# Who empties the bank of the deformable products: VectorE while it combines, or ScalarE behind the products

## The chip, the cores and the metric

The kernel runs on one core of one Trainium2 chip. The metric is the device time of one execution in microseconds (us); the kernel before took 9049.27 us in the median of three runs (9045.97 to 9068.44). Engines are named as the profile names them: PE is TensorE's matmul and PEld its weight load, DVE is VectorE, ACT is ScalarE, POOL is GpSimd, SP is SyncE, which only issues transfers. A `q` behind a name is the engine's sequencer.

## The reference, cut to what matters

Thirty-two images of 96 channels and 56 x 56 points go through two layers. The first is a hidden layer of 576 channels (1x1 convolution, 3x3 depthwise convolution, squeeze and excitation, 1x1 projection, residual). The second weights the image by a channel and a spatial attention, both drawn from its spectrum, and gives `y`. From `y` it computes offsets, a gate, an ordinary 3x3 convolution `y_base` and a deformable one, `y_def`. The part that the change touches is:

```python
sampled = _grid_sample_taps(y, px, py)
y_def = jnp.einsum('bcthw,oct->bohw', sampled, def_w.reshape(c, c, 9))
y_def = y_def + def_b[None, :, None, None]
z = (1 - gate) * y_base + gate * y_def
mu = z.mean((0, 2, 3), keepdims=True)
```

`z` is then normalised over all images, added to the layer's input and cut at zero. Everything is float32.

## The kernel before, in words

**Bands.** An image is cut into 7 bands of 8 rows, 448 points each, so that there are 224 bands. A band is worked in two halves of 7 tiles of 4 x 4 points, two tiles high (`h` = 0 and 1). For each half, sampling is done by products on TensorE (L739) of a transposed block of the image (`yt`, L721 to L727: copied by POOL, transposed by PE, emptied by ACT) with interpolation weights (`wc`, multiplied by DVE at L710 after two loads); ACT copies the results to `v` (L743) and packs two of the nine taps into the idle partitions (L750). Then `deform` (L758) multiplies `v` by the weights of the deformable convolution and adds up seven products in a bank of PSUM.

**The bank.** This bank is a pool of its own, `pd`, with one buffer. The first half of a band opens it, the second half adds its own columns, and then it holds all of the band's `y_def` without its bias. The other users of PSUM share six banks, `mm`, and one, `acc`. So the first products of the next band can't begin before `pd` has been read.

**The combining.** `combine` (L794 to L801) runs on DVE: L797 reads the bank, adds the bias `def_b` and subtracts `yb` (that is, `y_base`) in one instruction that writes `z`; L798 multiplies by the gate plus one; L799 halves and adds `yb`; L800 takes the statistics. `z` comes from a pool of two buffers. POOL stores it (L1061) later, and after the seventh band of an image DVE joins the statistics (L1068).

**The order of the work.** Beside the bands run two other streams: the hidden layer of the image after next (L169 to L262: expansions by PE emptied by ACT at L173, and depthwise taps, mostly on DVE at L262 and L260, closed by ACT at L222) and the attention of the next image (L285 to L587, with reductions on DVE at L379 and L437 that PE waits for at L440). `pump` advances both by a count of slots, 17 to a band, as their steps come due, and also runs what stands in the list `later` with a slot number. The offsets of the band after next (`find`: L615, L635, L637, L644, L649, L664 to L691) go along with them.

The end of a half isn't emitted where the half ends but in the next half, behind the first group of its sampling products: `ends` holds it. `end_half` emits `deform`, and after the second half it puts `join` into `later`, due two slots on. `join` calls `combine` and puts the store off by another seven slots.

What is emitted is not yet the order in which an engine works. When the kernel is built, the framework orders the instructions of each engine by an estimate of when each is ready, with earlier emission as the preference; SP's queue alone is kept as written. After that each engine works through its list strictly in order, and waits at an instruction whose operands or buffer are not there, whatever stands behind it.

Of the kernel before, what the change touches and what calls it, by code (L numbers as in the profile page):

```python
# [9 lines left out]
AF = mybir.ActivationFunctionType  # L10
ALU = mybir.AluOpType
# [5 lines left out]
C, H, W = 96, 56, 56  # L17
# [18 lines left out]
BW = NBW  # L36
# [81 lines left out]
def bank(p):  # L118
    return p["mm"].tile([128, 512], FP, name="mm")
# [485 lines left out]
def load_freq(nc, p, yp, b, r0, r1):  # L605
    nc.sync.dma_start(yp[CA - 1 : CA, PD + r0 : PD + r1, PD : PD + W], p["fq", b][:, r0:r1])


def conv3(nc, out, weights, yp, channels, j):

    view = out.rearrange("p (h w) -> p h w", h=RB)
    for k in range(NTAP):
        dy, dx = divmod(k, 3)
        r0 = j * RB + dy + PD - 1
        nc.tensor.matmul(view, weights[:, k], yp[:channels, r0 : r0 + RB, dx + PD - 1 : dx + PD - 1 + W],  # L615
                         start=(k == 0), stop=(k == NTAP - 1))
# [136 lines left out]
def deform(nc, p, pd, v, h):  # L753

    out = pd[:C, :BW].rearrange("c (q w) -> c q w", q=RB)[:, :, h * W // 2 : (h + 1) * W // 2]
    for k in range(KA):
        ks = slice(0, 128 if k else C)
        nc.tensor.matmul(out.rearrange("c q (t x) -> c t q x", x=TS), p["w"]["def"][ks, k],  # L758
                         v[ks, k].rearrange("c t s (r x) -> c t (s r) x", r=TS),
                         start=(k == 0), stop=(k == KA - 1))  # L760


def gate_of(nc, p, hid):

    pg = bank(p)
    nc.tensor.matmul(pg[:C, :BW], p["w"]["dg2"], hid, start=True, stop=True)
    return gate_from(nc, p, pg)


def gate_from(nc, p, pg):  # L770
    gate = p["q1"].tile([C, BW], FP, name="gate")
    nc.scalar.activation(gate, pg[:C, :BW], AF.Tanh, bias=p["w"]["half"]("dg2_b", C), scale=0.5)
    return gate
# [11 lines left out]
def base_conv(nc, p, j, yp):  # L785

    pb = bank(p)
    conv3(nc, pb[:C, :BW], p["w"]["base"], yp, C, j)
    yb = p["q1"].tile([C, BW], FP, name="yb")
    nc.scalar.activation(yb, pb[:C, :BW], AF.Identity, bias=p["w"]["cv"]("base_b"))  # L790
    return yb


def combine(nc, p, j, pd, yb, gate, st):  # L794

    z = p["q2"].tile([C, BW], FP, name="z")
    nc.vector.scalar_tensor_tensor(z, pd[:C, :BW], p["w"]["cv"]("def_b"), yb, ALU.add, ALU.subtract)  # L797
    nc.vector.scalar_tensor_tensor(z, gate, 1.0, z, ALU.add, ALU.mult)  # L798
    nc.vector.scalar_tensor_tensor(z, z, 0.5, yb, ALU.mult, ALU.add)  # L799
    nc.vector.bn_stats(st[:, j], z)  # L800
    return z  # L801
# [132 lines left out]
def padded(nc, p, a, images):  # L934

    cp = p["cp"]
    yps = [cp.tile([CJ, HY, WY], FP, name=f"yp{i}") for i in range(images)]
    for t in yps:
        nc.gpsimd.memset(t, 0.0)
        nc.sync.dma_start(t[C : C + 4, PD : PD + H, PD : PD + W], a["coord"])  # L940
        nc.sync.dma_start(t[CA:, PD : PD + H, PD : PD + W], a["place"])
    p["s4"] = [cp.tile([H, 3, WP], FP, name=f"s4_{i}") for i in range(2)]
    for t in p["s4"]:
        nc.gpsimd.memset(t, 0.0)
    return yps


def pools(tc, ctx, p, space, sizes):
    for name, bufs in sizes:
        kw = {"space": space} if space else {}  # L950
        p[name] = ctx.enter_context(tc.tile_pool(name=f"l1{name}", bufs=bufs, **kw))


def layers(tc, a, dp, x1d, zd, stats, far):
# [6 lines left out]
    nc = tc.nc  # L961
    B = x1d.shape[0]
    with ExitStack() as ctx:
        p = {"tc": tc, "dp": ctx.enter_context(tc.tile_pool(name="l1d", bufs=3, space=DRAM))}
# [3 lines left out]
        yp, = padded(nc, p, a, 1)  # L968
# [21 lines left out]
        streams, later = [], []  # L990
        slot = 0
# [68 lines left out]
        def store(b, j, z):  # L1060
            nc.gpsimd.dma_start(zd[b][:, j * BW : (j + 1) * BW], z)  # L1061

        def join(n, pd, gate, st):
            b, j = bands[n]
            z = combine(nc, p, j, pd, ybs[n], gate, st)
            later.append((slot + 7, lambda: store(b, j, z)))
            if j == NBD - 1:
                nc.vector.bn_aggr(stats[:, b], st)  # L1068

        def end_half(n, h, v, gate, st):  # L1070
            if h == 0:
                pds[n] = p["pd"].tile([128, 512], FP, name="pd")
            deform(nc, p, pds[n], v, h)
            if h:
                pd = pds.pop(n)
                later.append((slot + 2, lambda: join(n, pd, gate, st)))

        ends, pds = [], {}

# [9 lines left out]
        hids, gates, ybs, hds, ready = [], [], [], [], []  # L1089
# [31 lines left out]
        for n, (b, j) in enumerate(bands):  # L1121
            if j == 0:
                st = p["st"].tile([C, NBD, 6], FP, name="st")
# [7 lines left out]
            for h in range(2):  # L1131
# [20 lines left out]
                if h == 0:  # L1152
                    if n % 2 == 0:
                        gates.extend(gates_of(nc, p, hids[n // 2]))
                    gate = gates.pop(0)
# [108 lines left out]
def gather_block(tc, a, dp, x1d, zd, stats):  # L1264

    nc = tc.nc
    B = x1d.shape[0]
    sd = dp.tile([B, C, 2], FP, name="sd")
    with ExitStack() as ctx:
        p = {"dp": ctx.enter_context(tc.tile_pool(name="l1d", bufs=1, space=DRAM))}  # L1270
        pools(tc, ctx, p, PSUM, (("mm", 7), ("acc", 1)))
        constants(tc, ctx, a, p, True)
        yp, = padded(nc, p, a, 1)
        table = dp.tile([TAB, 4 * C], FP, name="table")
        with tc.tile_pool(name="l1z", bufs=1) as zp:
            zt = zp.tile([116, TAB * C // 116], FP, name="zt")
            nc.gpsimd.memset(zt, 0.0)
            tz = table.rearrange("(p n) f -> p (n f)", p=116)
            for i in range(4):
                nc.sync.dma_start(tz[:, i * zt.shape[1] : (i + 1) * zt.shape[1]], zt)  # L1280
        pools(tc, ctx, p, None, (("ca", 1), ("s1p", 1), ("xc", 2), ("sp", 1), ("sq", 2), ("hq", 1), ("q1", 2), ("q2", 2),
                                 ("hid", 2), ("off", 1), ("ix", 2), ("vp", 1), ("gp", 4), ("smp", 2)))
        with tc.For_i(0, B, 1) as b:
            st = p["sp"].tile([C, NBD, 6], FP, name="st")
            zo = p["dp"].tile([C, HW], FP, name="zo")
            xi = p["dp"].tile([C, HW], FP, name="xi")
            nc.sync.dma_start(xi.unsqueeze(0), x1d[bass.ds(b, 1)])
            for _ in attend(tc, p, 0, None, None, None, xi, True):
                pass
            for q in range(NB):  # L1290
                attend_table(nc, p, yp, table, xi, q)
            load_freq(nc, p, yp, 0, 0, H)
            for j in range(NBD):
                hid, wq, idx = locate(nc, p, yp, j)
                v = p["vp"].tile([C, NTAP, BW], FP, name="v")
                for t in range(GT):
                    sample_table(nc, p, table, wq, idx, v, t)
                pd = bank(p)
                for k in range(NTAP):
                    nc.tensor.matmul(pd[:C, :BW], p["w"]["def"][:, k], v[:, k], start=(k == 0), stop=(k == NTAP - 1))  # L1300
                z = combine(nc, p, j, pd, base_conv(nc, p, j, yp), gate_of(nc, p, hid), st)
                nc.sync.dma_start(zo[:, j * BW : (j + 1) * BW], z)
            mv = p["sp"].tile([C, 2], FP, name="mv")
            nc.vector.bn_aggr(mv, st)
            nc.sync.dma_start(zd[bass.ds(b, 1)], zo.unsqueeze(0))
            nc.sync.dma_start(sd[bass.ds(b, 1)].rearrange("o c n -> (o c) n"), mv)
    nc.sync.dma_start(stats, sd.rearrange("b c s -> c b s"))
# [50 lines left out]
@with_exitstack  # L1358
def body(ctx, tc, a, out):
    nc = tc.nc  # L1360
    B = a["x"].shape[0]
    dp = ctx.enter_context(tc.tile_pool(name="dram", bufs=1, space=DRAM))
    x1d = dp.tile([B, C, HW], FP, name="x1d")
    zd = dp.tile([B, C, HW], FP, name="zd")
    keep = ctx.enter_context(tc.tile_pool(name="keep", bufs=1))
    stats = keep.tile([C, B, 2], FP, name="stats")
    far = keep.tile([NOFF, 1], I32, name="far")
    with tc.manual_schedule(engines={mybir.EngineType.SP}):
        layers(tc, a, dp, x1d, zd, stats, far)

    reg = nc.values_load(far[0:1, 0:1], min_val=0, max_val=1)
    with tc.If(reg > 0):
        gather_block(tc, a, dp, x1d, zd, stats)
    normalise(tc, a, dp, [x1d[b] for b in range(B)], [zd[b] for b in range(B)], stats, out)
# [142 lines left out]
```

## Time and profile before

| what | value |
|---|---|
| median of three runs | 9049.27 us (9045.97 to 9068.44) |
| the profiled execution | 9059.03 us |
| its span, first to last instruction | 9057.2 us |
| mean granted clock of TensorE | 0.939 |
| L797, bank to `z` on DVE | 224 times, 665 / 680 / 690 ns (least, median, most) |
| L798, L799, L800 on DVE | 224 times each, medians 621, 614, 619 ns |
| L637 and L772 on ACT, bank to SBUF, 448 columns | 224 times each, 627 and 625 ns |
| DVE waiting at L797 for the products (L758) | 166.1 us in 64 waits, 8.1 at most |
| TensorE waiting at L758 for L797 | 115.6 us in 26 waits, 6.1 at most |
| TensorE busy, 1000 to 8000 us | 940 to 949 us of each 1000 |
| last product / end of span | about 8769 us / 9057 us |

How to read it: the span begins with some 500 us of constants and the first image, and ends with 285 us of normalisation, in which TensorE does nothing and transfers bound the time. Between them the same image step of about 264 us repeats, so that a view of one step (the timeline) stands for all, and totals over the span are divided by some 30 images. "Busy" is the time in which an engine had an instruction running; "idle before" is the time it stood still just ahead of a group of instructions, with the instruction that ended the wait. PEclk is the clock that TensorE was granted, 1.00 being the full one. In the page's second part each digit is the busy share of a fortieth of the span in tenths.

### The profile page before, as it was taken

The numbers are of one execution on the slowest core, as the hardware profiler recorded it, in microseconds if no ns is written. First come the engines' busy times: TensorE is split into PE (matmuls) and PEld (weight loads), VectorE is DVE, ScalarE is ACT, GpSimd is POOL, SyncE is SP. The second block draws the span as 40 slices with busy tenths as digits, with TensorE's granted clock in tenths as the row PEclk, the third lists the DMA queues.
The fourth block names the chain that finished last, engine by engine and source line by source line (L and its number), as shares of the span: only waits on it lengthen the run. The fifth ranks groups of instructions, "written<-read, shape, count | busy, mean of one in ns | idle before, by whom it ended". The sixth has DMA issues, their size and how long they took to land. (4 is left out here: it accounts for less than half of the span.)

```text
span 9057.2 us, 137476 instructions
## 1 busy us (share of the span) xinstructions
PE 8175.3 (90%) x52406; PEld 5193.5 (57%) x52406; DVE 7184.4 (79%) x6629; ACT 5393.5 (60%) x10486; POOL 2902.8 (32%) x2800
## 2 busy tenths in 40 slices
PE   5889999999999999999999999999999999999960
PEld 3456565665656566565656656565665655566640
DVE  7688888888888888888888888888888888888333
ACT  2356665666666666666666666666666666666553
POOL 0233333333333333333333333333333333333210
PEclk9889999999999999999999999999999999999985
DMA  2356666666666666666666666666666666666669
GB/s 82 108 142 160 163 169 165 157 154 153 163 166 171 166 157 147 158 165 164 172 161 154 159 157 168 165 174 161 154 154 160 165 166 172 166 156 144 144 188 416
DMA packets 1068758, 1486.48 MB, mean 164 GB/s; under 512 B 590191, under 2 KB 839839, under 8 KB 1055807
## 3 DMA queue, kind: packets, MB, share of 16 engines
q1 hardware_dynamic: 858995, 985.20, 46.4%
q10 hardware_dynamic: 153803, 329.80, 10.2%
q0 software_dynamic: 55296, 162.60, 6.7%
q8 instruction: 420, 6.88, 0.4%
q14 instruction: 244, 1.99, 0.1%
HBM read 1064.29 MB, written 412.65 MB: 163 GB/s over the span
## 5 line engine op out<-in xcount | busy, mean ns | idle before, releaser
L262 DVE SCALAR_TENSOR_TENSOR acch<-hp,w,acch 128x1512 f32<-128x1512 f32 (+1 forms) x2250 | 4456.4, 1981 | 141.4 <-ACT hp L173 103.8
L615 PE MATMUL mm<-yp,c_jointW 104*128 104x448 f32 x4032 | 1679.6, 568 | 10.1 <-DMA yp<-fqd 10.1
L758 PE MATMUL pd<-v,c_def 128*96 128x224 f32 (+1 forms) x6272 | 1468.8, 382 | 142.7 <-DVE z L797 115.6
L721 POOL COPY ybl<-yp 96x448 f32<-96x448 f32 x896 | 1048.3, 1198 | 1204.9 <-PE mm L725 1204.8
L758 PEld LDWEIGHTS pd<-v,c_def 128*96 128x96 f32 (+1 forms) x6272 | 1062.2, 176 | 449.8 <-issue 116.9
L615 PEld LDWEIGHTS mm<-yp,c_jointW 104*128 104x128 f32 x4032 | 776.6, 196 | 784.2 <-issue 747.4
L743 ACT COPY v<-mm 96x288 f32<-96x288 f32 (+1 forms) x2688 | 1004.3, 441 | 156.0 <-PE mm L739 109.3
L169 PE MATMUL mm<-xt,w 96*128 96x392 f32 (+3 forms) x2688 | 1058.5, 527 | 35.3 <-DMA xt<-in_x 33.1
L739 PE MATMUL mm<-wc,yt 64*96 64x144 f32 x12544 | 1056.9, 300 | 20.8 <-DVE sq L379 6.7
L739 PEld LDWEIGHTS mm<-wc,yt 64*96 64x96 f32 x12544 | 834.2, 164 | 317.3 <-issue 199.1
L173 ACT ACTIVATE hp<-mm,sh,inv 128x392 f32<-128x392 f32 (+2 forms) x1216 | 810.7, 673 | 344.8 <-PE mm L169 290.5
L710 DVE TENSOR_TENSOR wc<-wc,wr 128x1008 f32<-128x1008 f32 x448 | 566.6, 1265 | 412.5 <-DMA wr<-hd 385.1
L644 PE MATMUL mm<-yp,c_base0W 96*64 96x224 f32 x8064 | 830.1, 358 | 5.7 <-ACT hp L173 5.7
L329 PE MATMUL mm<-hq,w3s 128*96 128x392 f32 x2048 | 749.7, 510 | 63.6 <-DMA hq<-h2d 62.2
L672 POOL DMA_DIRECT2D od<-at x224 | 186.7, 834 | 1908.3 <-DVE at L664 1292.6
L750 ACT COPY v<-v 32x448 f32<-32x448 f32 x1344 | 755.1, 562 | 29.7
L727 ACT COPY yt<-mm 128x384 f32<-128x384 f32 (+1 forms) x896 | 353.9, 439 | 700.7 <-PE mm L725 699.0
L644 PEld LDWEIGHTS mm<-yp,c_base0W 96*64 96x64 f32 x8064 | 555.2, 135 | 282.7 <-issue 61.0
L635 ACT ACTIVATE hid<-mm,c_dg1b 50x448 f32<-50x448 f32 x224 | 140.8, 628 | 868.4 <-PE mm L615 858.4
L476 POOL TENSOR_TENSOR o<-o,xc 96x392 f32<-96x392 f32 x256 | 376.2, 1470 | 806.2 <-ACT o L339 804.2
L222 ACT ACTIVATE acch<-acch,sh,inv 128x1568 f32<-128x1568 f32 x288 | 488.4, 1696 | 202.8 <-DVE acch L262 176.5
L329 PEld LDWEIGHTS mm<-hq,w3s 128*96 128x96 f32 x2048 | 323.0, 166 | 395.2 <-issue 367.5
(194 smaller groups left out, 9325.3 us busy)
## 6 DMA issues: line engine op xcount, KB each, us to landing
h2d<-acch ACTq DMA_DIRECT2D x288, 784.0 KB
wc<-hd SPq DMA_DIRECT2D x896, 252.0 KB
wr<-hd SPq DMA_DIRECT2D x448, 504.0 KB
hq<-h2d SPq DMA_DIRECT2D x128, 980.0 KB
hq<-h2d SPq DMA_DIRECT2D x128, 784.0 KB
hq<-x1d SPq DMA_DIRECT2D x768, 98.0 KB
ht<-od SPq DMA_DIRECT2D x224, 252.0 KB
hd<-ho ACTq DMA_DIRECT2D x224, 252.0 KB
```

Source lines behind the costliest of these rows:

```text
L169: nc.tensor.matmul(pt[p0 : p0 + w1.shape[1], : rows * W], w1, xts[hf][:, r0 * W : (r0 + rows) * W], start=True, stop=True)
L173: nc.scalar.activation(h1[lo:hi, row0 : row0 + rows, 1 : 1 + W], pt[lo:hi, : rows * W].rearrange("p (h w) -> p h w", h=rows), AF.Silu, bia ...
L262: nc.vector.scalar_tensor_tensor(acc[:, lo:hi], win, wk, acc[:, lo:hi], ALU.mult, ALU.add)
L329: nc.tensor.matmul(pts[half][:C, :EW], w3s[:, ch], hq, start=(i == 0), stop=False)
L615: nc.tensor.matmul(view, weights[:, k], yp[:channels, r0 : r0 + RB, dx + PD - 1 : dx + PD - 1 + W], start=(k == 0), stop=(k == NTAP - 1))
L644: nc.tensor.matmul(pb[i * BC : (i + 1) * BC, : BW // 2].rearrange("p (h w) -> p h w", h=RB // 2), w["base"][:, k], yp[:C, r0 + i * RB // 2 ...
L710: p["tc"].keep_in_program_order(nc.vector.tensor_tensor(wc, wc, wr, ALU.mult))
L721: nc.gpsimd.tensor_copy(yb[:, :, s], blocks)
L739: nc.tensor.matmul(pt[k][:C, (t - lo) * KP : (t - lo + 1) * KP], yt[ps, t], s[ps, t * KP : (t + 1) * KP], start=True, stop=True)
L743: nc.scalar.copy(v[:C, :, lo:hi, k].rearrange("c k t p -> c t k p"), pt[k][:C, : (hi - lo) * KP].rearrange("c (t k p) -> c t k p", t=hi - ...
L750: nc.scalar.copy(v[C:, 1 + 2 * i : 3 + 2 * i], v[i * QC : (i + 1) * QC, KA:])
L758: nc.tensor.matmul(out.rearrange("c q (t x) -> c t q x", x=TS), p["w"]["def"][ks, k], v[ks, k].rearrange("c t s (r x) -> c t (s r) x", r=T ...
```

## The change

The reading of the bank is split off from `combine` and given to ScalarE, which adds the bias on the way and writes `z` in SBUF. It is emitted directly behind the products of the second half, no longer with the combining two slots later. `combine` finds `z` in SBUF and subtracts `yb` there, as a plain subtraction of two tiles in SBUF; its other three instructions stay. The slots of the combining and of the store stay as well. `z`'s buffer is taken two slots earlier than before. The second path, `gather_block`, which runs only when an offset is too large for the tiles (it doesn't with these inputs), gets the same two calls.

```diff
-def combine(nc, p, j, pd, yb, gate, st):
+def take(nc, p, pd):
 
     z = p["q2"].tile([C, BW], FP, name="z")
-    nc.vector.scalar_tensor_tensor(z, pd[:C, :BW], p["w"]["cv"]("def_b"), yb, ALU.add, ALU.subtract)
+    nc.scalar.activation(z, pd[:C, :BW], AF.Identity, bias=p["w"]["cv"]("def_b"))
+    return z
+
+
+def combine(nc, p, j, z, yb, gate, st):
+
+    nc.vector.tensor_tensor(z, z, yb, ALU.subtract)
     nc.vector.scalar_tensor_tensor(z, gate, 1.0, z, ALU.add, ALU.mult)
     nc.vector.scalar_tensor_tensor(z, z, 0.5, yb, ALU.mult, ALU.add)
     nc.vector.bn_stats(st[:, j], z)
...
-        def join(n, pd, gate, st):
+        def join(n, z, gate, st):
             b, j = bands[n]
-            z = combine(nc, p, j, pd, ybs[n], gate, st)
+            combine(nc, p, j, z, ybs[n], gate, st)
             later.append((slot + 7, lambda: store(b, j, z)))
...
             deform(nc, p, pds[n], v, h)
             if h:
-                pd = pds.pop(n)
-                later.append((slot + 2, lambda: join(n, pd, gate, st)))
+                z = take(nc, p, pds.pop(n))
+                later.append((slot + 2, lambda: join(n, z, gate, st)))
```

More of the change, by code (lines that the diff above doesn't have):

```diff
@@ L1300, in gather_block @@
                     nc.tensor.matmul(pd[:C, :BW], p["w"]["def"][:, k], v[:, k], start=(k == 0), stop=(k == NTAP - 1))
-                z = combine(nc, p, j, pd, base_conv(nc, p, j, yp), gate_of(nc, p, hid), st)
+                z = take(nc, p, pd)
+                combine(nc, p, j, z, base_conv(nc, p, j, yp), gate_of(nc, p, hid), st)
                 nc.sync.dma_start(zo[:, j * BW : (j + 1) * BW], z)
```

## The prediction

> **What bounds the kernel now.** I read the page first (busy shares and slices), then the list of waits of TensorE, then the timeline around the longest of them, then short windows with the granted clock.
>
> ```profile
> PE 8175.3 (90%) x52406; PEld 5193.5 (57%) x52406; DVE 7184.4 (79%) x6629; ACT 5393.5 (60%) x10486; POOL 2902.8 (32%) x2800
> ...
> PE   5889999999999999999999999999999999999960
> ...
> DVE  7688888888888888888888888888888888888333
> ```
>
> From the fourth slice to the last but two TensorE is busy nine tenths or more (windows of 1000 us between 1000 and 8000 give 940 to 949), VectorE eight tenths; ScalarE has 616 to 636 of each 1000. TensorE is the bound, and what can be won is its idle time of 50 to 60 us in each 1000, and time in which its clock is low. The waits of TensorE, columns total us, times, longest:
>
> ```profile
> PE pd L758 <- DVE z L797: 115.6, 26, 6.1
> PE acc L440 <- DVE m_fy L437: 72.8, 30, 5.6
> PE acc L440 <- DVE m_fe L437: 71.1, 31, 2.5
> PE mm L329 <- DMA hq<-h2d: 62.2, 31, 4.2
> PE mm L725 <- DVE at L664: 57.2, 28, 5.7
> PE pd L758 <- ACT v L743: 19.3, 36, 2.8
> ```
>
> The largest is the one that the change touches: the first product of a new band waits until VectorE's L797 has read the only bank of `pd`. It strikes 26 times in 224 bands, about once per image. The timeline shows one (start, duration, engine):
>
> ```profile
> 4748.53 2.81 PE L758 MATMUL pd<-v,c_def 96*96 96x224 f32 x14
> ...
> 4751.71 0.78 ACT L727 COPY yt<-mm 128x384 f32<-128x384 f32 x2 [2.25 <-PE mm L725]
> ...
> 4752.44 1.21 DVE L710 TENSOR_TENSOR wc<-wc,wr 128x1008 f32<-128x1008 f32 x1 [4.91 <-DMA wr<-hd]
> ...
> 4753.56 5.92 DVE L262 SCALAR_TENSOR_TENSOR acch<-hp,w,acch 128x1568 f32<-128x1568 f32 x3
> ...
> 4756.18 1.74 ACT L750 COPY v<-v 32x448 f32<-32x448 f32 x3
> ...
> 4759.52 0.68 DVE L797 SCALAR_TENSOR_TENSOR z<-pd,c_cvec,yb 96x448 f32<-96x448 f32 x1
> ...
> 4760.25 1.06 PE L758 MATMUL pd<-v,c_def 96*96 96x224 f32 x2 [3.80 <-DVE z L797]
> ...
> 4761.74 4.42 PE L758 MATMUL pd<-v,c_def 128*96 128x224 f32 x12
> ```
>
> The old band's products end at 4751.34. VectorE first waits 4.91 us for a load, then runs L710 and three taps of 5.92 us, and reads the bank only at 4759.52; TensorE has stood still for 3.80 us. And there is a second price. The 14 products at 4748.53 took 2.81 us, 0.201 each; the 12 behind the stall took 4.42, 0.368 each. The windows tell why (length, then busy time by engine, then PEclk, the granted clock):
>
> ```profile
> 4754.00:4756.45 2.45, 2.45 (x18) 1.23 (x18) 2.42 (x2) 2.42 (x4) 0.07 (x1) 1.00 0.51 103
> 4756.45:4760.25 3.80, 0.00 (x0) 0.00 (x1) 3.68 (x3) 3.73 (x8) 0.00 (x0) 0.83 1.02 318
> 4760.25:4766.00 5.75, 5.75 (x19) 4.52 (x20) 5.63 (x10) 0.72 (x2) 0.52 (x1) 0.52 1.00 211
> ```
>
> Clock 1.00 before, 0.83 over the stall, 0.52 over the next 5.75 us of full work: the stall halves the clock and work behind it pays.
>
> **The change part by part.** *The stall.* The bank is now freed by one ScalarE instruction, emitted directly behind the products and not two slots later. In the example ScalarE had 2.25 us free until 4751.71, and the products end at 4751.34 in that gap: the copy would run from about 4751.4 to 4752.0 and push the row behind it by 0.34. TensorE, idle from 4756.45, needs for the next products only `v`. Its first tap uses rows written by L743 long before; the taps behind it need L750, which ends at 4757.92 for all three packs, 4758.3 with the push, the first pack over a microsecond earlier; four transposes stand in between. I leave 0.5 us of the stall per place. 26 waits give 115.6 - 13 = 103 us.
>
> *The clock behind it.* I laid 27 windows of 14 us at these places, 1305 to 8194. TensorE is idle for 114.9 of their 378 us. Their clocks are 0.76 seventeen times, 0.88 twice, 0.63 to 0.67 eight times, mean 0.733: half clock for (1 - 0.733) x 2 x 378 = 202 us, 7.5 per place. In the example 1.3 of its 6.8 us of half clock lie in the stall and 5.5 in work, which at 0.368 for 0.201 holds 3.0 us of full-clock work: 2.5 us lost. Scaled by 7.5/6.8 to 27 places: some 70 us. It goes if the stall goes, since in the window before it the clock is 1.00. Together 103 + 70 = 173 us, 6.4 per image.
>
> *ScalarE's new work.* 224 instructions from PSUM, 96 x 448 with a bias. Nearest row: L637, the same operation with 32 x 448, 627 ns; L772 with 96 x 448, 625. So 224 x 0.63 = 141 us on an engine that is idle for 37% of the steady part. Identity with a bias is used by L637, L649 and L339 today, and no table load (131 in all, 1283 ns) stands at those lines, so I add none. On the path: the copy is emitted just ahead of the second group of L743, on which L758 waits 36 times already. All waits of TensorE for ScalarE sum to about 75 us in some 70 times. Bounds: nothing, and 141 if each copy delays TensorE in full. I take 20, which lengthens 70 such waits by 0.3 each, since most lines of ScalarE wait for TensorE themselves (L635 858 us, L727 699).
>
> *VectorE.* L797 goes (680 ns in the median), a subtraction with both operands in SBUF comes.
>
> ```profile
> L798 DVE SCALAR_TENSOR_TENSOR z<-gate,z 96x448 f32<-96x448 f32 x224 | 196.1, 876 | 3.7
> L799 DVE SCALAR_TENSOR_TENSOR z<-z,yb 96x448 f32<-96x448 f32 x224 | 152.2, 679 | 2.4
> L797 DVE SCALAR_TENSOR_TENSOR z<-pd,c_cvec,yb 96x448 f32<-96x448 f32 x224 | 152.2, 679 | 170.3 <-PE pd L758 166.1
> ```
>
> L798 and L799 read both operands from SBUF: median 621 and 614, yet up to 1870 and 970; L797 reads one from PSUM and stays within 665 to 690 in all 224. So the subtraction costs VectorE between 224 x (614 - 680) = -15 and 224 x (876 - 679) = +44 us; I take L799's mean, which gives nothing. This row is where a rule speaks against the change: "SBUF — State Buffer" of the Trainium skill, section "Who interferes with whom", says that a VectorE instruction with two SBUF inputs contends with a GpSimd instruction that reads SBUF, one blocking the other, while one with a single SBUF input does not. By the rule the subtraction becomes like L798 and the sum is worse by what part of 44 us reaches TensorE; by L799 it is unchanged. The spreads above agree with the rule.
>
> VectorE also waits differently: 64 times, 166.1 us, it stood at L797 for the products; now it stands some 0.7 us longer, 45 us in all. None of this holds the bank any more, and nothing of VectorE's z chain is read by TensorE; what it delays is what is queued behind it (L262, L437, L664). The store on POOL (L1061) waits for L799 as before and has nothing urgent behind it: z has two buffers and is written some 38 us apart, so taking it two slots earlier costs nothing.
>
> *What is late next.* With 6.4 us gained per image TensorE comes sooner to its other waits for VectorE. Behind the stall VectorE is busy 42.18 of 50 us (4760 to 4810), then 82.01 of 90 (to 4900), then 66.60 of 86. So it has 7.8 + 8.0 us of slack up to the place where L725 waits for L664 and L440 for L437, of which part is waiting for loads, that do not come sooner. There some of the lead is lost. Bounds: nothing given back, and all. VectorE's slack to 4986 is 35 us against 6.4 wanted, nearer to nothing, but the tight stretch (4810 to 4900) comes first: I take 40%, 70 us.
>
> **Sum.** -103 - 70 + 20 + 0 + 70 = -83 us. The profiled execution took 9059.0 (span 9057.2 and 1.8 around it), 9.8 above the median of 9049.3; so 8976 for it and 8966 by the median.
>
> **Rivals.** *(a) All of it arrives.* Nothing is given back and ScalarE's copies are hidden: 9049 - 173 = 8876. For: VectorE's slack over a whole image; against: 91% in the tight stretch. 0.2.
>
> *(b) The bank comes no earlier, or the next wait takes it all.* The order on each engine is fixed when the program is built, by estimates. If the copy is put behind L222, L750 and the gates (until 4759.1 in the example), the bank is free at 4759.8, as late as now; or L437 and L664 hand back everything. Then 9049 - 173 + 173 and 0 to 20 of copies: about 9050 to 9070, say 9055. Against: the copy's emission ahead of those lines. 0.12.
>
> *(c) Slower: ScalarE blocks in front of the products.* ScalarE works in order. If its queue reaches the copy before the products are done, it stands, and behind it stand the emptyings of the six banks of `mm` (L743, L727, L173), for which TensorE waits next. VectorE shows how often the queue is early: 64 times, 166.1/64 = 2.6 us each. The price is 64 x (2.6 + 0.63) = 207 us if nothing hides it, against the 103 won with the rest given back: from half of it reaching TensorE the change loses. In full 9049 - 103 + 207 = 9153; at two thirds, which I take for it, 9049 - 103 + 138 = 9084. For: the products of one half stretch to over 16 us in some bands, interleaved with other work. Against: ScalarE stands 858 us at L635 today and TensorE does not mind. 0.13.
>
> **How the numbers follow.** The forecast, 8966, has a chance of 0.55, (a) 0.2, (b) 0.12, (c) 0.13. Its own range by the unknown costs is 8920 to 9020. The range from 8870 to 9085 takes in (a) and (b) and (c) at two thirds, and leaves out about 0.15: (c) in full, and a new order of all queues, which any edit brings. A measurement here tells apart about 0.3%, 27 us. Faster by more than that: (a), and nearly all of the forecast: 0.74. Within: (b) and the forecast's edge: 0.12. Slower: (c) and a little of (b): 0.14.
>
> **What would show it.** The wait of L758 for z must vanish from TensorE's list, and the one for the new copy be under 20 us; the clock over the steady part rise from 0.96 (0.95 to 0.96 in windows of 1000 us) to 0.97 or more; ScalarE's busy time rise by 141. The give-back shows as larger waits of L440 and L725 for VectorE. A new line of ScalarE waiting for L758 with over 150 us, and L743 among the first that TensorE waits for, is (c). The prediction is wrong if the stalls go and the time stays.

## The result and the profile after

The kernel after takes 8973.95 us in the median of four runs (8964.88 to 8983.66), the kernel before beside it 9051.45 (9045.97 to 9068.44): a ratio of 0.9911, 95% interval 0.9893 to 0.993. That is 78 us less; the forecast was 83 less. The profiled execution took 8980.98 us, against 9059.03 before. Its busy shares, and TensorE's waits (total us, times, longest):

```profile
PE 8127.0 (91%) x52406; PEld 5153.6 (57%) x52406; DVE 7147.7 (80%) x6629; ACT 5486.5 (61%) x10710; POOL 2988.3 (33%) x2800
```

```profile
PE acc L440 <- DVE m_fe L437: 70.6, 31, 2.5
PE acc L440 <- DVE m_fy L437: 70.6, 29, 8.9
PE mm L739 <- DVE sq L379: 59.8, 29, 3.5
PE mm L329 <- DMA hq<-h2d: 57.8, 30, 3.8
...
PE mm L725 <- POOL ybl L721: 39.6, 37, 3.0
...
PE pd L758 <- ACT v L743: 23.9, 34, 1.3
PE mm L396 <- DVE sq L379: 20.6, 17, 2.5
...
PE mm L725 <- DVE at L664: 7.8, 10, 1.4
```

Two things are to be seen. The wait of L758 for the bank, 115.6 us before, is gone without a successor of its own. And three waits have grown most: for L379 (6.7 before, all at L739), for POOL's L721 (1.0 before) and, lower in the list, L615 for a load (30.5, before 10.1). The same work of TensorE, 52406 products, takes 8127.0 us instead of 8175.3; by the clock records of the two traces, 565 us of it ran at half clock, before 702.

The place of the old stall, in the timeline (the combining's lines are now L803 to L806, the copy is L797):

```profile
4698.17 2.81 PE L758 MATMUL pd<-v,c_def 96*96 96x224 f32 x14
...
4701.02 0.63 ACT L797 ACTIVATE z<-pd,c_cvec 96x448 f32<-96x448 f32 x1 [1.92 <-PE pd L758]
...
4702.17 1.90 DVE L710 TENSOR_TENSOR wc<-wc,wr 128x1008 f32<-128x1008 f32 x1 [4.24 <-DMA wr<-hd]
...
4703.99 5.61 DVE L262 SCALAR_TENSOR_TENSOR acch<-hp,w,acch 128x1568 f32<-128x1568 f32 x3
...
4705.93 0.54 PE L758 MATMUL pd<-v,c_def 96*96 96x224 f32 x2
...
4706.64 2.44 PE L758 MATMUL pd<-v,c_def 128*96 128x224 f32 x12
```

VectorE has a like load wait and the same three taps in front of it, but ScalarE has the bank empty at 4701.65, in the gap ahead of L727. The next products start at 4705.93 with no wait, and the twelve take 2.44 us, not 4.42. Some 30 us on, a new one stands (two windows: length, busy times, granted clock):

```profile
4735.62 1.83 DVE L262 SCALAR_TENSOR_TENSOR acch<-hp,w,acch 128x1568 f32<-128x1568 f32 x1
...
4737.48 0.62 DVE L379 TENSOR_REDUCE sq<-mm 112x56 f32<-112x448 f32 x1
...
4738.16 1.14 PE L739 MATMUL mm<-wc,yt 64*96 64x144 f32 x8 [2.27 <-DVE sq L379]
```

```profile
4736.00:4738.16 2.16, 0.00 (x0) 0.00 (x0) 2.13 (x3) 0.62 (x2) 2.16 (x3) 1.00 0.36 85
4738.16:4742.00 3.84, 3.84 (x24) 3.07 (x28) 2.96 (x4) 2.36 (x6) 0.22 (x1) 0.52 0.61 152
```

L379 reduces squares out of a bank of `mm`; it is queued behind a tap, and L739 needs that bank. Here 2.27 us and the clock's halving are paid again. The list above has 29 waits of this kind, about one per image. So the stall was in part exchanged for a shorter one.

### The profile page after: what moved, and what is told of

It is laid out like the page before. It is cut to its first block, busy times and chain, and to the rows that moved or that the text cites. A ratio compares the mean times of both kernels' runs of the same rounds, so it can differ in the third digit from the quotient of the medians.

```text
span 8979.2 us, 137810 instructions
## 1 busy us (share of the span) xinstructions
PE 8127.0 (91%) x52406; PEld 5153.6 (57%) x52406; DVE 7147.7 (80%) x6629; ACT 5486.5 (61%) x10710; POOL 2988.3 (33%) x2800
## 5 line engine op out<-in xcount | busy, mean ns | idle before, releaser
L615 PE MATMUL mm<-yp,c_jointW 104*128 104x448 f32 x4032 | 1669.5, 565 | 31.5 <-DMA yp<-fqd 30.5
L721 POOL COPY ybl<-yp 96x448 f32<-96x448 f32 x896 | 1137.6, 1297 | 1080.7 <-PE mm L725 1080.4
L758 PE MATMUL pd<-v,c_def 128*96 128x224 f32 (+1 forms) x6272 | 1400.0, 369 | 25.6 <-ACT v L743 23.9
L615 PEld LDWEIGHTS mm<-yp,c_jointW 104*128 104x128 f32 x4032 | 772.1, 195 | 802.8 <-issue 764.5
L758 PEld LDWEIGHTS pd<-v,c_def 128*96 128x96 f32 (+1 forms) x6272 | 1024.7, 170 | 304.3 <-issue 82.1
L739 PE MATMUL mm<-wc,yt 64*96 64x144 f32 x12544 | 1053.3, 298 | 73.2 <-DVE sq L379 59.8
L743 ACT COPY v<-mm 96x288 f32<-96x288 f32 (+1 forms) x2688 | 1004.1, 443 | 116.8 <-PE mm L739 91.2
L739 PEld LDWEIGHTS mm<-wc,yt 64*96 64x96 f32 x12544 | 827.3, 162 | 367.4 <-issue 194.3
L710 DVE TENSOR_TENSOR wc<-wc,wr 128x1008 f32<-128x1008 f32 x448 | 586.3, 1309 | 403.9 <-DMA wr<-hd 377.5
L750 ACT COPY v<-v 32x448 f32<-32x448 f32 x1344 | 755.2, 562 | 29.6
L169 PEld LDWEIGHTS mm<-xt,w 96*128 96x128 f32 (+1 forms) x2688 | 363.0, 179 | 327.8 <-issue 222.5
```

The lines of the kernel that those rows point to most:

```text
L169: nc.tensor.matmul(pt[p0 : p0 + w1.shape[1], : rows * W], w1, xts[hf][:, r0 * W : (r0 + rows) * W], start=True, stop=True)
L710: p["tc"].keep_in_program_order(nc.vector.tensor_tensor(wc, wc, wr, ALU.mult))
L721: nc.gpsimd.tensor_copy(yb[:, :, s], blocks)
L739: nc.tensor.matmul(pt[k][:C, (t - lo) * KP : (t - lo + 1) * KP], yt[ps, t], s[ps, t * KP : (t + 1) * KP], start=True, stop=True)
L743: nc.scalar.copy(v[:C, :, lo:hi, k].rearrange("c k t p -> c t k p"), pt[k][:C, : (hi - lo) * KP].rearrange("c (t k p) -> c t k p", t=hi - ...
L750: nc.scalar.copy(v[C:, 1 + 2 * i : 3 + 2 * i], v[i * QC : (i + 1) * QC, KA:])
```

## The experiments

My theory: the change wins because the only bank of `pd` no longer waits for VectorE's late queue, and what is lost again is lost where VectorE is late with another bank. Rivals: the earlier emission does it, whichever engine reads; or it is no more than a new order of the queues, which any edit brings.

### Which engine, or which moment

`dve_behind`, the kernel before with VectorE's reading emitted directly behind the products:

```diff
             if h:
-                pd = pds.pop(n)
-                later.append((slot + 2, lambda: join(n, pd, gate, st)))
+                z = take(nc, p, pds.pop(n), ybs[n])   # L797's instruction, on VectorE
+                later.append((slot + 2, lambda: join(n, z, gate, st)))
```

> The kernel before, with VectorE's reading of the bank (pd plus bias minus yb, one instruction) emitted directly behind the products and the rest of the combining two slots later as before. The engine stays, only the moment moves. Theory 'engine' (the bank came late because VectorE's queue runs late, and ScalarE's doesn't): the wait of L758 for z stays above 60 us, time 9000 to 9060. Rival 'moment' (the earlier emission alone frees the bank): the wait falls under 30 us, time 8990 or less.

Measured: 9196.76 us, ratio 1.0167 (1.0151 to 1.0182). Neither expectation held. The wait of L758 for `z` is gone, as the rival said, and yet the time is 1.7% longer. VectorE now reaches L797 too early and stands there for the products (the first line), and TensorE has a new wait (the second):

```profile
DVE z L797 <- PE pd L758: 351.7, 97, 8.0
...
PE mm L739 <- ACT v L750: 99.9, 51, 4.9
```

Before, these were 166.1 us in 64 waits and 5.9 us in two. What is queued behind L797 comes late, and TensorE pays for it: at the old place L739 starts at 4808.17 after 2.37 us of standing, 0.10 behind the end of L710 (4806.88, 1.19 long), which multiplies its weights and follows L797 on VectorE. (The list puts this wait down to ScalarE's L750.) TensorE's busy time also rose, from 8175.3 to 8263.1 us. This is the mechanism of rival (c) of the prediction, on VectorE.

`act_late`, the kernel after with ScalarE's copy emitted with the combining, two slots later:

```diff
-                z = take(nc, p, pds.pop(n))
-                later.append((slot + 2, lambda: join(n, z, gate, st)))
+                pd = pds.pop(n)
+                later.append((slot + 2, lambda: join(n, pd, gate, st)))   # join calls take
```

> The kernel after, with ScalarE's copy of the bank emitted with the combining, two slots later. The engine is changed, the moment isn't. Theory 'engine': the wait of L758 for the copy stays under 20 us, and the time within 25 us of the kernel after (8950 to 9000). Rival 'moment': the wait comes back with over 60 us, time 9010 to 9060.

Measured: 8976.61 us, ratio 0.9923 (0.991 to 0.9936); no wait of L758 for the copy. These are the numbers of theory 'engine', but the run is no test of the moment, for the planner put the copy back:

```profile
4711.40 0.63 ACT L797 ACTIVATE z<-pd,c_cvec 96x448 f32<-96x448 f32 x1 [1.92 <-PE pd L758]
4711.93 0.76 ACT L727 COPY yt<-mm 128x384 f32<-128x384 f32 x2
```

It stands where it stood in the kernel after, behind the same 1.92 us of waiting for the products and ahead of L727. So it is in nearly every band: ahead of L727 189 times, in the kernel after 191, and in both kernels 0.04 us behind the last product in the median. `act_late` is thus the kernel after once more. What a later copy on ScalarE would cost stays open; that an earlier reading doesn't help on VectorE is what `dve_behind` shows.

### Freeing the bank without ScalarE, and ScalarE without freeing the bank

`two_banks` and its control `five_banks`:

```diff
-        pools(tc, ctx, p, PSUM, (("mm", 6), ("acc", 1), ("pd", 1)))
+        pools(tc, ctx, p, PSUM, (("mm", 5), ("acc", 1), ("pd", 2)))   # control: 5, 1, 1
```

> The kernel before with two banks for the deformable products and five for the rest instead of one and six; VectorE empties them as before. To be read against five_banks. Theory 'the bank' (what the change wins is that the next products need not wait for VectorE): the wait of L758 for z is under 15 us, half clock is less, and the time is 60 to 110 us below five_banks. Rival 'a new order of the queues, or VectorE's shorter work': within 20 us of five_banks.

> Control for two_banks: the kernel before with five banks of mm instead of six, and one for the deformable products; one bank of PSUM lies idle. Both theories: the wait of L758 for z stays at 90 to 140 us; the time is 0 to 80 us above the kernel before (9050 to 9130), by waits for mm banks.

Measured: `five_banks` 9013.84 us, ratio 0.9959 (0.9943 to 0.9975); `two_banks` 8998.44, ratio 0.9954 (0.9939 to 0.9968). Two surprises. With a bank less for everything else the kernel was not slower but 0.4% faster, although its L758 still waits 95.9 us for `z`. And freeing the bank on top won 15 us, nothing that the intervals can tell apart, although that wait is gone; the rival expected this, my theory 60 to 110. Where it went:

```profile
PE mm L739 <- DVE sq L379: 44.2, 19, 5.3
...
PE mm L615 <- DVE sq L379: 34.2, 16, 3.6
```

In `five_banks` these are 10.3 and 0.9. So in the profiled executions (that of `two_banks` is the fastest of its six) 67 of 96 us came back at L379's banks, as in the kernel after.

`both_read`, the kernel before with ScalarE's copy added; VectorE reads the bank as well and overwrites `z`:

```diff
+    nc.scalar.activation(z, pd[:C, :BW], AF.Identity, bias=p["w"]["cv"]("def_b"))   # behind the products
...
     nc.vector.scalar_tensor_tensor(z, pd[:C, :BW], p["w"]["cv"]("def_b"), yb, ALU.add, ALU.subtract)
```

> The kernel before, with ScalarE's copy of the bank into z added behind the products as in the kernel after; VectorE then reads the bank itself as before and writes z anew. ScalarE's work of the change is there, the early release of the bank isn't. Theory 'the bank': the wait of L758 for VectorE's z stays at 80 to 140 us, half clock as before, time 9040 to 9100 (ScalarE's 141 us cost 0 to 50). Rival 'a new order' (the gain comes from how the queues fall out once ScalarE has these rows): 8960 to 9010 although the bank is held.

Measured: 9094.47 us, ratio 1.0055 (1.0042 to 1.0068), with

```profile
PE pd L758 <- DVE z L803: 112.8, 28, 5.9
```

Time and wait lie where my theory put them. ScalarE's new work with the bank still held costs 43 us. The gain is not ScalarE's presence in the order; between this kernel and the one after, 120 us apart, lie the release of the bank and the simpler first instruction of VectorE.

### What order alone can do

`before_slot3` and its pair `after_slot3`, and `after_slot4`: the combining is due three (four) slots behind the products.

```diff
-                later.append((slot + 2, lambda: join(n, pd, gate, st)))
+                later.append((slot + 3, lambda: join(n, pd, gate, st)))
```

> The kernel before with the combining due three slots behind the products and not two: an edit that frees nothing sooner. It samples what a new order alone can do, since five banks in place of six made the kernel faster by 0.4%. Theory 'the bank': the bank is freed later, the wait of L758 grows from 116 to 130 to 250 us, time 9060 to 9150. Rival 'a new order': anything within 60 us of the kernel before on either side, with no relation to that wait.

> The kernel after, with the combining due three slots behind the products and not two; ScalarE's copy stays directly behind the products. The pair to before_slot3 (9004), which won 47 us by order alone with the stall still there at 121 us. Theory 'the bank': the stall's worth comes on top, 50 to 110 us below before_slot3: 8895 to 8955. Rival 'a new order' (the change won its 78 us by an order of the same kind, and both can't be had): within 25 us of the kernel after or slower, 8960 or more.

> The same with four slots. Theory 'the bank': z has nothing waiting for it but the store, so the time stays within 40 us of after_slot3, and the wait of L758 for the bank stays under 20 us. Rival 'a new order': anywhere from 8900 to 9050, with the spread that three slots against two had.

Measured: `before_slot3` 9004.14 us, 0.9951 (0.9938 to 0.9964), against my theory: it wins 47 us while L758 waits 120.7. Its waits of L440 for L437 (m_fy) are 10.7 us, before 72.8, but others grew as much, POOL's L721 from 1.0 to 62.1; the gain is in TensorE's busy time, 8124.6 us against 8175.3. `after_slot3` takes 8968.09, 0.9901 (0.9885 to 0.9918), `after_slot4` 8969.58, 0.9901 (0.9885 to 0.9917). Between the two with three slots the release is worth 36 us by the medians (45 by the ratios), half of the 78 at two slots, and less than the 50 that I asked of the bank: the rival's line, 8960 or more, is the one that held. `after_slot4` stays as near to `after_slot3` as theory 'the bank' said (no wait of L758 for the bank), but it lies in the rival's range too. `after_slot3` is the fastest median of all, but its interval overlaps with that of the kernel after.

### Where the rest went back

`squares`, the kernel after with L377's squares in SBUF, and `before_squares`, the same edit of the kernel before:

```diff
-        sq = bank(p)[: 2 * H, : CG * W].rearrange("h (c w) -> h c w", c=CG)
+        sq = p.get("o", p["xc"]).tile([2 * H, W, CG], FP, name="o").rearrange("h w c -> h c w")
```

> The kernel after, with the squares of L377 written to a tile in SBUF (channels innermost) and not to a bank of mm; VectorE reduces them from there. So no bank of the six waits for VectorE's L379 any more. Theory 'handed back' (what the freed bank won was partly lost where VectorE, running late, holds mm banks at L379): the waits of L739 and L396 for L379, 80 us together, go, and 30 to 80 us are won: 8895 to 8945. Rival 'VectorE itself is late' (another wait for it takes their place, L437, L664 or POOL's L721): within 25 us of the kernel after.

> Control for squares: the kernel before with the same edit. There L379 cost TensorE 7 us. Theory 'handed back': the wait of L758 for z stays over 80 us and the time within 40 us of the kernel before. Rival 'the squares' banks matter by themselves': 40 to 100 us faster than before.

Measured: 9056.32 us, 1.0012 (1.0 to 1.0025), and 9069.48, 1.0028 (1.0017 to 1.004). Neither expectation of `squares` held. The waits for L379 did go, but the edit is no clean test. L377, writing rows with the channels innermost, takes 1030 ns instead of 547, it waits 129.9 us for loads at a worse place of ScalarE's queue (9.9 in the kernel after), and stalls of mostly 3 to 5 us stand near the old place again, now put down to ScalarE:

```profile
PE pd L758 <- ACT v L743: 80.4, 51, 5.0
...
PE mm L739 <- ACT v L743: 49.2, 16, 4.8
```

In `before_squares` the time is as expected, but L758's wait for `z` fell to 53.0 us, not the 80 or more of the theory. `squares` does show that ScalarE, once late itself, gives the stall back. What L379's banks cost remains read from waits alone.

`no_sub` leaves the subtraction out; `one_input` puts in its place statistics of `z`, with one operand:

```diff
-    nc.vector.tensor_tensor(z, z, yb, ALU.subtract)
+    idle = p["q1"].tile([C, 6], FP, name="idle")   # no_sub: neither line
+    nc.vector.bn_stats(idle, z)
```

> The kernel after without the subtraction L803, which it leaves out: 181 us less work for VectorE. Theory 'VectorE runs late behind each image's end and hands back the gain': the waits of TensorE for L379 fall from 80 to under 40 us and the time to 8900 to 8950. Rival 'VectorE has slack and the rest is order and loads': within 20 us of the kernel after.

> The kernel after, with the subtraction L803 replaced by statistics of z alone into an idle tile: one operand from SBUF in place of two, the same 448 elements. What it leaves out: the subtraction. Theory 'a second operand from SBUF is what slows it and POOL's copies' (L803 took 807 ns in the mean, up to 1556; POOL's L721 rose from 1198 to 1297): the new row stays within 560 to 640 ns, L721 falls to 1150 to 1230 ns; the time within 30 us of the kernel after, since POOL is a small limit (L725 waits 40 us for L721). Rival 'L721 rose because of the order': it stays at 1270 or more, L804 meets POOL instead.

Measured: `no_sub` 8991.87 us, 0.993 (0.9916 to 0.9944): without L803 (181 us; VectorE's busy time fell by 142) nothing was won, and the waits for L379 stayed (55.4 at L396, 39.6 at L739), as the rival said. So VectorE does not hand back the gain by having this work to do. That it does so by what stands ahead of L379 in its queue is read from the one place above, not tested. `one_input` 8984.44, 0.9922 (0.9909 to 0.9936). Its rows, columns busy us and mean ns, beside L803 of the kernel after:

```profile
L804 DVE BATCH_NORM_STATS2 idle<-z 96x6 f32<-96x448 f32 x224 | 138.2, 617 | 226.7 <-ACT z L797 226.7
```

```profile
L803 DVE TENSOR_TENSOR z<-z,yb 96x448 f32<-96x448 f32 x224 | 180.8, 807 | 226.5 <-ACT z L797 226.2
```

The row with one operand from SBUF is 190 ns shorter in the mean (603 to 641 each, against 604 to 1556 with two). The operation differs too, but the traces settle which it is. In the kernel after, 97 of the 224 L803 overlap no copy or arithmetic of POOL, and none of them takes more than 632 ns; all 86 that take over 660 overlap one. With one operand from SBUF, L804 of `one_input` overlaps one 132 times and L797 of the kernel before 105 times, and none takes more than 690. That agrees with what "SBUF — State Buffer" of the Trainium skill says in "Who interferes with whom", that a VectorE instruction with two inputs in SBUF contends with a GpSimd instruction that reads SBUF. But the time doesn't follow it: nothing was won, and POOL's L721 went from 1297 ns only to 1260, where neither expectation had it. In `no_sub`, which leaves the row out, it took 1403, so it goes by more than this operand.

## Why the prediction was right

**The stall.** Forecast 103 us of 115.6, half a microsecond left at each place; all went. The copy ran where it was put, in ScalarE's gap ahead of L727, and the wait for L743, the next operand, rose only from 19.3 to 23.9.

**The clock.** Forecast 70 us, measured 48.3 in TensorE's busy time for the same products; the mean granted clock rose from 0.939 to 0.949, and over the steady part (1000 to 8000 us) from 0.96 to 0.97. The mechanism holds: L758's own products took 68.8 us less (before, after; busy us, mean ns, idle before).

```profile
L758 PE MATMUL pd<-v,c_def 128*96 128x224 f32 (+1 forms) x6272 | 1468.8, 382 | 142.7 <-DVE z L797 115.6
...
L758 PE MATMUL pd<-v,c_def 128*96 128x224 f32 (+1 forms) x6272 | 1400.0, 369 | 25.6 <-ACT v L743 23.9
```

What the forecast left out is that new stalls halve the clock again: the products of the attention, L396 and L420, took 47 us more, and by the clock records they ran at half clock for 117 us, before for 18 (L758: 135, before 276). But busy time can also fall with the bank still held: `before_slot3` has 50.7 us less of it with the stall at 120.7.

**ScalarE's work.** Forecast 141 us busy and 20 on the path. The copy took 627 ns in the mean, 140.3 us in all, though ScalarE's busy time rose by 93 only (5486.5 against 5393.5). ScalarE stood at it 143 times for 236.7 us, far oftener than the 64 of VectorE from which rival (c) was priced, and all waits of TensorE for ScalarE still fell from 77.5 to 64.6 us. With the bank held the same work cost 43 us, twice the 20; since a new order alone moves as much, the 20 itself was not measured.

**VectorE's work.** Forecast nothing. The subtraction is dearer than L797 (807 ns for 679), but the next two are cheaper (686 for 876, 624 for 679): the three together fell from 2234 to 2117 ns, 26 us in all. The first of the three overlaps POOL's work most often (L803 127 times, the other two 114 and 41), and the first one used to be L797, which reads one operand from PSUM and is not slowed by it. The 45 us that VectorE was to stand longer at the first one came to 60 (226.2 against 166.1).

**Given back.** Forecast 70 us of 173, at L440 and L725 waiting for VectorE. Measured: TensorE's time outside its work went from 9057.2 - 8175.3 = 881.9 to 8979.2 - 8127.0 = 852.2 us, 29.7 less, so that 85.9 of the 115.6 came back. The places were wrong: L440 lost as much as before and L725 waits 49 us less for L664; it came back at L379's banks (+78, 84.7 against 6.7), at POOL's L721 (+39) and at a load (+20). The sum, -115.6 - 48.3 + 85.9 = -78.0, stands against the -83 that was forecast, ScalarE's 20 within the last term. That the two come within 5 us is in part luck: the stall was 13 us larger and the clock 22 us smaller than forecast, and an order alone, below, moves the time by more.

**What the prediction missed.** It named a new order of all queues only as what the range leaves out. The runs show it to be as large as a term of the sum: two edits that free nothing won 29 and 47 us by the medians, one that adds only work lost 43. Seven kernels in which L758 never waits for the reader of its bank, nor for a late ScalarE, lie from 8968 to 8998 us; the kernel before, `five_banks`, `before_slot3` and `both_read`, in which it waits 96 to 121 us, from 9004 to 9094. But six of the seven are the kernel after and its variants. The only one that frees the bank in another way, `two_banks`, is not told apart from `five_banks` and `before_slot3` (ratios 0.9954, 0.9959, 0.9951). `dve_behind` and `squares` show that the wait must not be moved to TensorE's other operands.

What freeing the bank does at L758 is shown in four pairs: the wait of 96 to 121 us goes, and L758's own products take 69, 57 (`five_banks` and `two_banks`), 49 (three slots) and 63 us less (`both_read` and the kernel after). What the rest of TensorE's work gives back differs from pair to pair, and so what share of the 78 us is the bank's alone can't be settled: the times of these pairs differ by 78, 15 (not told apart from nothing), 36 and 120 us, and `squares` and `before_squares`, where the wait moved to ScalarE, by 13.

## What to carry to other kernels

When a single buffer ties a fast engine to a late queue, try to let that engine empty it whose queue waits for the fast one anyway; here, moving the same read earlier in the late queue only made that queue stand. After the stall goes, look for the next buffer that the late queue holds, and expect a good part of the gain to reappear there. When a planner lays out the queues anew after each edit, see in the trace whether the edit moved what it was to move (in `act_late` it didn't), and take two or three neighbouring variants of both kernels before a difference of up to one per cent is put down to the edit.

## What the runs showed of the hardware

A stall of 2.27 us was enough to halve TensorE's clock: the window behind it, 3.84 us of full work, has 0.52. It need not: of the 41 stalls of 2.25 to 2.5 us that began at full clock in the kernel after (1000 to 8000 us), 33 had the clock halved by 3.4 us behind their end. "TensorE: Matmul & The Clock Gate" of the Trainium skill, in Part 1, ties the low clock to an idle window of about 3.4 us; here the measurement decides, and shorter stalls count too. And ScalarE's activation of 112 x 448 took 547 ns into PSUM, but 1030 into SBUF with a step of eight elements between neighbours; no run separates the memory from the step.
